# Attention and a mixture of experts on one core: when the last tokens' routing pieces are put between the expert matmuls

## The chip, the cores and the metric

The kernel runs on one core of a Trainium2 chip. A core has five engines with an instruction queue each: TensorE (matmuls; the profile writes PE, and PEld for its weight loads), VectorE (DVE), ScalarE (ACT), GpSimd (POOL) and SyncE (SP), which here issues transfers. An engine works through its queue in order; engines wait for each other by semaphores. The metric is the device time of one execution in microseconds, lower is better. Several executions are timed, and their median is compared; one further execution is recorded by the hardware profiler.

## The reference

Input is x of shape 8 x 1024 x 256, all in float32. There are two layers, each with a residual:

```python
x = x + layernorm(attention(layernorm(x)))      # 16 heads of 16, causal
x = x + layernorm(experts(layernorm(x)))

def experts(h):                                  # h: 8192 tokens x 256
    scores = softmax(h @ router_weight.T + router_bias)      # 8 experts
    topk_w, topk_idx = top_k(scores, 2)
    gu = einsum('th,ehn->ten', h, gate_up_proj) + gate_up_bias   # 2 x 512 columns
    gate, up = minimum(gu[..., :512], 7), clip(gu[..., 512:], -7, 7)
    act = (up + 1) * gate * sigmoid(1.702 * gate)
    down = einsum('tei,eih->teh', act, down_proj) + down_bias
    return weighted sum of the two chosen experts' rows of down
```

## The kernel before

**Two stages.** Attention goes through the 8 batches, 4 groups of heads each. Its output is projected, normalized and added per block of 512 tokens; there are 16 blocks (0 to 15), two for each batch. After it comes the expert stage. It computes only the chosen (token, expert) pairs: each token's normalized row is scattered to two rows of a table in DRAM (`xsd`), in which each expert has a region, and the expert stage reads this table in 71 tiles of 256 rows (`NTILES`), each belonging to one expert.

**The way of a block of tokens** (`finish`, L867, and `route`, L927 to L1052): output projection, normalization, residual; a second normalization to `xn`; transposes on TensorE (`x2ps`, L944), copied by ScalarE; the router's matmuls (`lpsT`, L951), a copy, a transpose (`lps`, L959); the softmax and the ranks of the experts on VectorE (L961 to L1001) ending in `is_r` and `chosen`; a matmul that counts the chosen ahead of each token (`cps`, L1005); ten small operations on VectorE that turn counts into rows (`counted`, `slot`, `counts`); then eight indirect scatters by GpSimd (L1046). For batch 7 (`last`), blocks 14 and 15, some pieces use other engines and other distances.

**The tables.** Which expert and which rows tile i takes is made on the chip (`table`, L279 to L366) from the counts: once from the first 12 blocks, for the first 12 tiles (`EARLY`), and once from all 16 for the rest. The second begins when block 15 is counted, after `fill_tails` (L252) has had the unused end of each expert's region filled with zeros: SyncE reads eight row numbers and issues eight transfers (L260). Then come the table's matmuls `segps` (L311), `firstps` (L319) and `tabps` (L343), each between small operations of VectorE. So the expert stage starts on rows of the first 12 blocks while batch 7's blocks are still on their way beside it.

**The order of work is written out.** TensorE, VectorE and ScalarE run in the order of the source, and GpSimd's instructions are held to it too. Side work is made of generators that yield pieces, each with its cost in us by engine and a distance:

```python
def piece(pe=0.0, dve=0.0, act=0.0, pool=0.0, after=0):
    return (pe, dve, act, pool), after
```

`pump(pe, dve, act, pool)` adds these amounts to a credit for each engine (capped at 0.9, GpSimd's at 1.3), then emits pieces whose engines are not in debt, and counts `now` up by one. A piece with `after=n` is not taken before n pumps have gone by since the piece ahead of it was emitted. The main loop of the expert stage calls `pump` three times in each quarter of a tile, as long as i + 2 < 12. At i = 10, `finish_all` emits what is left.

**An expert tile** (`quarter`, L1303; `lower_half`, L1335; loop L1453). A tile has four quarters (f = 0 to 3), of 128 gate and 128 up columns each: eight matmul records `gu` (L1308) into one of four PSUM buffers, with the first pump after half of them. VectorE makes `gate` (L1317) and `up` (L1321), ScalarE the sigmoid `sig` (L1319), GpSimd multiplies sig by gate (L1324); then the second pump. The product `act` (L1329) of the quarter before is issued on VectorE after that (`left()`), so that it is a quarter behind; after it stand the other work of the quarter and the third pump:

```python
                now_left = quarter(i, f, xT, wg, bs, act)
                if left:
                    left()
                left = now_left
```

After quarter 1 and after quarter 2 comes half of the previous tile's down product (`dn`, L1339), which needs its four `act`; after quarter 2 also the transposes of the next tile (`xtps`, L1288) and the operation `ys` (L1345) that empties `dn`. GpSimd scatters the result's rows (L1349).

**Loads.** SyncE loads tile i + 2 when tile i begins: its rows (`xs`, L1264), gate and up weights (`wg`, L1268; three buffers), biases (L1272) and down weights (L1276). The rows' load waits for the scatters into `xsd` that stand ahead of it in the source. The zeros stand in SyncE's queue between the loads of tile 9 and tile 10.

Side work and dn share three PSUM buffers (`ps_b`).

Of the kernel before, what the change touches and what calls it, by code (L numbers as in the profile page):

```python
# [24 lines left out]
def piece(pe=0.0, dve=0.0, act=0.0, pool=0.0, after=0):  # L25


    return (pe, dve, act, pool), after
# [30 lines left out]
def attn_moe_kernel(  # L59
# [179 lines left out]
    def ahead_of(load, group):  # L239

        tc.add_to_no_dep_group(group, load.ins)
# [37 lines left out]
    def table(nr):  # L279

        yield piece(dve=0.8)
        first_ones = nr < NT
# [22 lines left out]
        if first_ones:  # L305
            nc.vector.memset(new[:, nr:, :], 0.0)

        yield piece(pe=0.6, dve=0.2, after=3)
        ps = ps_b.tile([P, 2], F32, tag="b", name=f"segps_{nr}")
        for k, v in enumerate((new, nf[:, :NT, :])):  # L310
            nc.tensor.matmul(  # L311
# [26 lines left out]
        two = tp.tile([P, 2, NTILES], F32, tag="two", name=f"two_{nr}")  # L338
        nc.vector.tensor_scalar(two[:, 0, :], mine, seg_e, None, ALU.mult)
        nc.vector.scalar_tensor_tensor(two[:, 1, :], itile, at, mine, ALU.add, ALU.mult)  # L340
        yield piece(pe=0.5, dve=0.6, after=2)
        ps = ps_b.tile([P, 2, NTILES], F32, tag="b", name=f"tabps_{nr}")
        nc.tensor.matmul(  # L343
            ps.rearrange("o k i -> o (k i)"), lhsT=ones,
# [63 lines left out]
    with ExitStack() as attn:  # L408
# [123 lines left out]
        def others(wr):  # L532

            rwr, gubr = wr["r"], wr["gub"]

            nc.sync.dma_start(
                out=xs_dram[ds(E * R, TS), :].rearrange("(n p) d -> p n d", p=P), in_=zeros
            )
            for name in ("v", "o"):
                for kt in range(KT):  # L540
                    yield piece(pe=0.3, act=0.45)
                    weights(name, wr[name], kt)
            yield piece(pe=0.3, dve=0.2)
            ps = ps_b.tile([P, KT, E], F32, tag="b", name="rps")
            for kt in range(KT):
                nc.tensor.transpose(ps[:, kt, :], rwr[:, ts(kt, P)], ident[:E, :E])
            nc.vector.tensor_copy(rw32[:, :, :E], ps)
            yield piece(pe=0.2, dve=0.4)
            ps = ps_b.tile([P, E * 2 * FT], F32, tag="b", name="gubps")
            nc.tensor.transpose(ps, gubr, ident[: E * 2 * FT, : E * 2 * FT])  # L550
            bias = ap2.tile([P, E, 2 * FT], F32, tag="lgT", name="bias")
            nc.vector.tensor_copy(bias, ps.rearrange("p (e c) -> p e c", e=E))

            nc.vector.tensor_scalar(bias[:, :, FT:], bias[:, :, FT:], 1.0, None, ALU.add)
            nc.sync.dma_start(
                out=bias_dram[:, :, : 2 * FT].rearrange("e p c -> p e c"), in_=bias
            )
            for e in range(E):
                nc.sync.dma_start(
                    out=bias_dram[e, :, 2 * FT :], in_=down_b[e].partition_broadcast(P)  # L560
                )
# [365 lines left out]
        def route(t, x1, last):  # L927
# [10 lines left out]
            more = 1 if last else 0  # L938
# [5 lines left out]
                    nc.tensor.transpose(ps[:, n, :], xn[:, n, ts(kt, P)], ident)  # L944
                nc.scalar.copy(xT[:, kt, :], ps.rearrange("p n c -> p (n c)"))

            yield piece(pe=0.6, act=0.3, after=1 + more)
            ps = ps_b.tile([P, P], F32, tag="b", name=f"lpsT_{t}")
            for kt in range(KT):
                for n in range(NTB):  # L950
# [48 lines left out]
            for r in range(TOPK):  # L999
                nc.vector.tensor_scalar(is_r[:, r], rank, float(r), None, ALU.is_equal)  # L1000
            nc.vector.tensor_scalar(chosen, rank, float(TOPK), None, ALU.is_lt)  # L1001
            yield piece(pe=0.6, dve=0.2, after=1 + more)
            cps = ps_b.tile([P, 2, NTB, E], F32, tag="b", name=f"cps_{t}")
            for k, m in enumerate((before, ones)):
                nc.tensor.matmul(  # L1005
# [11 lines left out]
            for n in range(NTB):  # L1017
                nc.vector.tensor_tensor(slot[:, n, :], slot[:, n, :], so_far, ALU.add)
                after = counts[:, nth + 1, :]
                if n + 1 < NTB:  # L1020
                    after = small.tile([P, E], F32, tag="after", name="after")
# [43 lines left out]
        def start(kind, gen):  # L1065
            job = Job(gen, now)
            kind.append(job)
            return job
# [12 lines left out]
        def earn(*us):  # L1081
            for i, more in enumerate(us):
                credit[i] = min(credit[i] + more, 1.3 if i == 3 else 0.9)
# [9 lines left out]
        def spend(least=0.0, most=9.0):  # L1093


            found = affordable(least, most)
            if found:
                kind, job = found
                found = job.cost
                for i, cost in enumerate(job.cost):  # L1100
                    credit[i] -= cost
                emit(kind, job)
            return found

        def pump(*us, most=9.0):

            nonlocal now
            earn(*us)
            while True:
                got = spend(most=most)  # L1110
                if not got:
                    break

                if got[0] >= 0.3 and most <= 1.0:
                    most = min(most, 0.29)
            now += 1
# [22 lines left out]
        with tc.manual_schedule(  # L1139
# [5 lines left out]
            more = start(due, others(wr))  # L1145
# [157 lines left out]
    def quarter(i, f, xT, wg, bs, act):  # L1303

        ps = ps_gu.tile([P, 2, TS], F32, tag="gu", name=f"gu_{i}_{f}")
        for half in range(2):
            for kt in range(KT):
                nc.tensor.matmul(  # L1308
                    ps[:, half, :],
                    lhsT=wg[:, kt, ds(half * FF + f * P, P)],  # L1310
                    rhs=xT[:, kt, :],
                    start=(kt == 0), stop=(kt == KT - 1),
                )
            if half == 0 and i + AHEAD < EARLY:
                pump(0.6, 0.35, 0.6, 0.35)
        gt = m3.tile([P, TS], F32, tag="gate", name=f"gate_{i}_{f}")
        nc.vector.tensor_scalar(gt, ps[:, 0, :], bs[:, f : f + 1], LIMIT, ALU.add, ALU.min)  # L1317
        sg = m3.tile([P, TS], F32, tag="sig", name=f"sig_{i}_{f}")
        nc.scalar.activation(sg, gt, AF.Sigmoid, scale=ALPHA)  # L1319
        up = m3.tile([P, TS], F32, tag="up", name=f"up_{i}_{f}")  # L1320
        nc.vector.tensor_scalar(  # L1321
            up, ps[:, 1, :], bs[:, FT + f : FT + f + 1], LIMIT + 1.0, ALU.add, ALU.min
        )
        in_order(nc.gpsimd.tensor_tensor(sg, sg, gt, ALU.mult))  # L1324
        if i + AHEAD < EARLY:
            pump(0.6, 0.35, 0.6, 0.35)

        def product():
            nc.vector.scalar_tensor_tensor(  # L1329
                act[:, f, :], up, 1.0 - LIMIT, sg, ALU.max, ALU.mult  # L1330
            )

        return product
# [100 lines left out]
    with tc.manual_schedule(engines={engines.PE, engines.DVE, engines.Activation}):  # L1434
        free[0] = False
        loads = {0: load_tile(0)}
        for i in range(IN_X, 2 * IN_X):
            at = loaded(tables[NT - LATE][:, 1, i : i + 1], E * R)
            early[i] = m4.tile([P, TN, XD], F32, tag="xs", name=f"xs_{i}")
            ahead_of(nc.sync.dma_start(out=early[i], in_=slot_rows(at)), "xs")  # L1440
        for i in range(1, AHEAD):
            loads[i] = load_tile(i)
        xTs = {0: turned(0, loads[0][0])}
        behind, left = None, None
        waiting = deque()
        ready = 0
        ends = deque()

        def an_end(i):
            if ends and i >= ends[0][0] and next(ends[0][1], "end") == "end":  # L1450
                ends.popleft()

        for i in range(NTILES):  # L1453
            if i + AHEAD == EARLY:
                finish_all()
            if i + AHEAD < NTILES:
                loads[i + AHEAD] = load_tile(i + AHEAD)
            _, wg, bs, wd = loads.pop(i)
            xT = xTs.pop(i)
            act = m2.tile([P, FT, TS], F32, tag="act", name=f"act_{i}")  # L1460
            for f in range(FT):
# [4 lines that stand above are left out]
                for _ in range(2 if f == FT - 1 and i % 2 else 1):  # L1466
                    an_end(i)
                if f == 1 and behind:
                    next(behind)
                if f == 2:  # L1470
                    if i + 1 < NTILES:
                        xTs[i + 1] = turned(i + 1, loads[i + 1][0])
                    if behind:
                        next(behind)
                        next(behind)
                if i + AHEAD < EARLY:
                    pump(1.2, 0.7, 1.0, 0.7)
            while ready < NT and i >= tiles_for(ready):
                waiting.append(ready)
                ready += 1  # L1480
            if waiting and len(ends) < 2:
                work = both(routed[waiting.popleft()])
                next(work)
                ends.append((i + 2, work))
            behind = lower_half(i, act, wd, bs)
        left()
        for _ in behind:
            pass
        for r in [*waiting, *range(ready, NT)]:
            ends.append((0, both(routed[r], r == NT - 1)))  # L1490
        while ends:
            an_end(NTILES)
        free[0] = True
# [36 lines left out]
```

## Time and profile before

| what | value |
|---|---|
| median of 3 runs | 2231.09 us (2227.67 to 2233.11) |
| the profiled execution | 2227.21 us |
| its span, first to last instruction | 2225.5 us |
| TensorE busy | 2161.5 us, 97% of the span, 16801 matmul records |
| VectorE busy | 1647.3 us, 74% |
| ScalarE busy | 1090.8 us, 49% |
| GpSimd busy | 1067.0 us, 48% |
| expert stage's first `gu` | 1405.4 us from the span's start |
| `gu`, 2272 matmul records | 516.2 us, 379 ns each |
| `dn`, 1136 matmul records | 273.5 us, 381 ns each |
| scatters to `xsd`, 128 | 126.9 us, 992 ns each |

A busy time is the sum of the recorded durations on one engine, and matmul records overlap: one of 379 ns can be followed by the next after about 216 ns. Lines in order of time give start, duration, engine, line, operation, output and input, shape and count; what stands in brackets at the end is the engine's idle time ahead of it and what ended it. A wait's row names who waited for whom, the sum, how often, and the longest.

### The profile page before, as it was taken

The numbers are of one execution on the slowest core, as the hardware profiler recorded it, in microseconds if no ns is written. First come the engines' busy times: TensorE is split into PE (matmuls) and PEld (weight loads), VectorE is DVE, ScalarE is ACT, GpSimd is POOL, SyncE is SP. The second block draws the span as 40 slices with busy tenths as digits, with TensorE's granted clock in tenths as the row PEclk, the third lists the DMA queues.
The fourth block names the chain that finished last, engine by engine and source line by source line (L and its number), as shares of the span: only waits on it lengthen the run. The fifth ranks groups of instructions, "written<-read, shape, count | busy, mean of one in ns | idle before, by whom it ended". The sixth has DMA issues, their size and how long they took to land.

```text
span 2225.5 us, 45180 instructions
## 1 busy us (share of the span) xinstructions
PE 2161.5 (97%) x16801; PEld 1347.5 (61%) x16801; DVE 1647.3 (74%) x3770; ACT 1090.8 (49%) x2179; POOL 1067.0 (48%) x1229
## 2 busy tenths in 40 slices
PE   7999999999999999999999999999999999999995
PEld 3444544544544445445445444778888888888885
DVE  4776777867867777877776787676668888887775
ACT  3666665665666666666666666431122322322222
POOL 3421652662573573473472463464444444444543
PEclk9999999999999999999999999999999999999998
DMA  4001102102102111111111111657667778777773
GB/s 106 17 12 35 26 16 55 40 21 59 40 21 55 36 30 38 52 30 31 49 40 23 45 52 40 219 178 253 214 227 269 259 262 273 266 243 273 241 245 124
DMA packets 141363, 251.17 MB, mean 113 GB/s; under 512 B 17664, under 2 KB 103576, under 8 KB 139224
## 3 DMA queue, kind: packets, MB, share of 16 engines
q1 hardware_dynamic: 126968, 212.17, 30.5%
q0 software_dynamic: 12960, 35.54, 4.2%
q8 instruction: 133, 2.18, 0.4%
q14 instruction: 86, 0.70, 0.1%
q10 hardware_dynamic: 1216, 0.58, 0.1%
HBM read 175.74 MB, written 55.76 MB: 104 GB/s over the span
## 4 chain that ended last, share of the span: by engine, by line
PE 81%; DVE 10%; POOL 4%; issue 3%; ACT 1%; DMA 1%; SPq 0%; ACTq 0%; DVEq 0%; POOLq 0%
PE sa L693 20%; PE gu L1308 17%; PE av L825 12%; PE dn L1339 9%; PE sb L788 7%; PE yps L886 3%; PE pjq L600 3%; PE pjk L600 3%; PE vps L586 2%; PE avt L856 1%; DVE acc L1391 1%; PE xtps L1288 1%; DVE gate L1317 1%; DVE act L1329 1%; DVE up L1321 1%
## 5 line engine op out<-in xcount | busy, mean ns | idle before, releaser
L796 ACT ACTIVATE pT<-sb 128x512 f32<-128x512 f32 x1152 | 625.2, 595 | 404.5 <-PE sb L788 375.7
L788 PE MATMUL sb<-qP,kP 32*128 32x512 f32 (+3 forms) x3072 | 710.7, 523 | 2.1 <-DMA qP<-nmT 1.0
L693 PE MATMUL sa<-kP,qP 32*128 32x512 f32 (+3 forms) x3072 | 653.8, 524 | 3.4 <-DVE mx L703 1.4
L1308 PE MATMUL gu<-xsT,wg 128*128 128x256 f32 x2272 | 516.2, 379 | 0.8 <-ACT xsT L1290 0.7
L1308 PEld LDWEIGHTS gu<-xsT,wg 128*128 128x128 f32 x2272 | 430.6, 190 | 59.9 <-ACT xsT L1290 1.4
L805 POOL TENSOR_SCALAR_AFFINE_SELECT pT<-pT 128x512 f32<-128x512 f32 x256 | 160.0, 641 | 592.3 <-ACT pT L796 586.9
L709 DVE TENSOR_REDUCE mx<-sa 128x2 f32<-128x1024 f32 x256 | 311.5, 1219 | 112.2 <-PE sb L788 108.6
L1319 ACT ACTIVATE sig<-gate 128x256 f32<-128x256 f32 x284 | 118.3, 417 | 562.7 <-DVE gate L1317 560.7
L825 PE MATMUL av<-pT,vpad 128*32 128x256 f32 (+1 forms) x5120 | 345.0, 366 | 1.1 <-DVE avs L836 0.9
L1324 POOL TENSOR_TENSOR sig<-sig,gate 128x256 f32<-128x256 f32 x284 | 210.6, 743 | 274.9 <-ACT sig L1319 273.0
L693 PEld LDWEIGHTS sa<-kP,qP 32*128 32x128 f32 x3072 | 227.8, 184 | 188.4 <-issue 97.3
L788 PEld LDWEIGHTS sb<-qP,kP 32*128 32x128 f32 x3072 | 297.6, 184 | 40.9 <-ACT pT L796 7.2
L825 PEld LDWEIGHTS av<-pT,vpad 128*32 128x32 f32 x5120 | 116.4, 108 | 287.2 <-issue 208.0
L1339 PE MATMUL dn<-wd,act 128*128 128x256 f32 x1136 | 273.5, 381 | 8.0 <-DVE act L1329 7.5
L1317 DVE TENSOR_SCALAR gate<-gu,bs 128x256 f32<-128x256 f32 x284 | 135.7, 478 | 154.2 <-PE gu L1308 138.1
L1339 PEld LDWEIGHTS dn<-wd,act 128*128 128x128 f32 x1136 | 208.6, 190 | 40.7 <-DVE act L1329 16.0
L703 DVE CUSTOM_DVE_ANT_0 sa<-sa,cmask 128x512 f32<-128x512 f32 x256 | 178.1, 697 | 51.2 <-PE sb L788 27.0
L1349 POOL DMA_INDIRECT ytd<-ys,places x142 | 142.9, 1006 | 136.5 <-DVE ys L1345 112.3
L1046 POOL DMA_INDIRECT xsd<-xn,slots x128 | 126.9, 992 | 47.0 <-issue 29.4
L718 DVE TENSOR_REDUCE mx<-sa 128x2 f32<-128x512 f32 x128 | 88.1, 689 | 75.5 <-PE sb L788 49.7
L1329 DVE SCALAR_TENSOR_TENSOR act<-up,sig 128x256 f32<-128x256 f32 x284 | 131.7, 464 | 14.5 <-POOL sig L1324 14.5
L1321 DVE TENSOR_SCALAR up<-gu,bs 128x256 f32<-128x256 f32 x284 | 134.5, 474 | 0.0
(204 smaller groups left out, 2399.9 us busy)
## 6 DMA issues: line engine op xcount, KB each, us to landing
wg<-_L_ffn_gate_up_proj_dram SPq DMA_DIRECT2D x71, 1024.0 KB
wd<-in_L_ffn_down_proj_dram SPq DMA_DIRECT2D x71, 512.0 KB
xs<-xsd SPq DMA_DIRECT2D x67, 258.0 KB
yy<-ytd SPq DMA_DIRECT2D x15, 1024.0 KB
bs<-biasd SPq DMA_DIRECT2D x71, 132.0 KB
x<-in_L_attn_x_dram SPq DMA_DIRECT2D x16, 512.0 KB
x1d<-y SPq DMA_DIRECT2D x16, 512.0 KB
x<-x1d SPq DMA_DIRECT2D x16, 512.0 KB
```

Source lines behind the costliest of these rows:

```text
L693: nc.tensor.matmul(ps[:, hh, ds(at, w)], lhsT=qP[r, ts(i, P)], rhs=kP[r, ds(c * QC, w)], start=True, stop=True,)
L703: nc.vector.tensor_tensor_reduce(out=ps[:, hh, :], in0=ps[:, hh, :], in1=cmask, scale=1.0, scalar=NEG, op0=ALU.add, op1=ALU.max, accum_out ...
L709: nc.vector.tensor_reduce(mx[:, heads, i, 2:3], ps, AX.X, ALU.max)
L788: nc.tensor.matmul(banks[hh][:, ds(at, QC - off)], lhsT=kP[r, ts(j, P)], rhs=qP[r, ds(c * QC + off, QC - off)], start=True, stop=True,)
L796: nc.scalar.activation(pT[:, 2 * pair + hh, :], banks[hh], AF.Exp)
L805: in_order(nc.gpsimd.affine_select(out=d, in_=d, compare_op=ALU.is_ge, fill=0.0, base=0, pattern=[[0, HG], [1, P]], channel_multiplier=-1,))
L825: nc.tensor.matmul(av[ds(hh * HS, HS), ds(off + a - at, z - a)], lhsT=vp[:, j, ds((g * HG + hh) * VS, HS)], rhs=pT[:, hh, a:z],  start=c n ...
L1308: nc.tensor.matmul(ps[:, half, :], lhsT=wg[:, kt, ds(half * FF + f * P, P)], rhs=xT[:, kt, :], start=(kt == 0), stop=(kt == KT - 1),)
L1317: nc.vector.tensor_scalar(gt, ps[:, 0, :], bs[:, f : f + 1], LIMIT, ALU.add, ALU.min)
L1321: nc.vector.tensor_scalar(up, ps[:, 1, :], bs[:, FT + f : FT + f + 1], LIMIT + 1.0, ALU.add, ALU.min)
L1324: in_order(nc.gpsimd.tensor_tensor(sg, sg, gt, ALU.mult))
L1339: nc.tensor.matmul(ps[:, n, :], lhsT=act[:, f, ts(n, P)], rhs=wd[:, f, :], start=(f == 0), stop=(f == FT - 1),)
```

## The change

Six numbers change, and with them the order in which the pieces of blocks 14 and 15 and of the second table are emitted. For `last` blocks the router's matmul `lpsT` gets a distance of 3 pumps instead of 2, and `cps` 5 instead of 2; for the second table `segps` gets 5 instead of 3 and `tabps` 5 instead of 2. Other blocks and the first table keep theirs. Of the three pumps of a quarter, the two inside `quarter` add nothing to VectorE's credit (0.35 each before), and the third, after the product, adds 1.4 instead of 0.7. No instruction is added or removed.

```diff
 def table(nr):
-        yield piece(pe=0.6, dve=0.2, after=3)
+        yield piece(pe=0.6, dve=0.2, after=3 if first_ones else 5)
         ps = ps_b.tile([P, 2], F32, tag="b", name=f"segps_{nr}")
...
-        yield piece(pe=0.5, dve=0.6, after=2)
+        yield piece(pe=0.5, dve=0.6, after=2 if first_ones else 5)
         ps = ps_b.tile([P, 2, NTILES], F32, tag="b", name=f"tabps_{nr}")
...
 def route(t, x1, last):
-            yield piece(pe=0.6, act=0.3, after=1 + more)
+            yield piece(pe=0.6, act=0.3, after=1 + 2 * more)
             ps = ps_b.tile([P, P], F32, tag="b", name=f"lpsT_{t}")
...
-            yield piece(pe=0.6, dve=0.2, after=1 + more)
+            yield piece(pe=0.6, dve=0.2, after=1 + 4 * more)
             cps = ps_b.tile([P, 2, NTB, E], F32, tag="b", name=f"cps_{t}")
...
 def quarter(i, f, xT, wg, bs, act):
             if half == 0 and i + AHEAD < EARLY:
-                pump(0.6, 0.35, 0.6, 0.35)
+                pump(0.6, 0.0, 0.6, 0.35)
...
         if i + AHEAD < EARLY:
-            pump(0.6, 0.35, 0.6, 0.35)
+            pump(0.6, 0.0, 0.6, 0.35)
...
                 if i + AHEAD < EARLY:
-                    pump(1.2, 0.7, 1.0, 0.7)
+
+                    pump(1.2, 1.4, 1.0, 0.7)
```

## The prediction

> **What bounds the kernel now.** I read the page's slices first, then the waits of TensorE in the stretch that the change reaches, then the rows in order of time of TensorE, VectorE and GpSimd there. The page, TensorE's share of the 40 slices and the chain that ended last:
>
> ```profile
> PE   7999999999999999999999999999999999999995
> ...
> PE 81%; DVE 10%; POOL 4%; issue 3%; ACT 1%; DMA 1%; SPq 0%; ACTq 0%; DVEq 0%; POOLq 0%
> ```
>
> TensorE is the bound throughout, so the change is worth what TensorE waits less. The instructions differ only between the expert stage's start (1405 us) and tile 10 (about 1534 us); before and after it, every engine has the old order. TensorE's waits from 1395 to 1545 us (line, who ended it, sum, times, longest):
>
> ```profile
> PE cps L1005 <- DVE chosen L1001: 3.1, 2, 2.1
> PE dn L1339 <- DVE act L1329: 2.9, 3, 1.4
> PE tabps L343 <- DVE two L340: 2.1, 1, 2.1
> PE segps L311 <- DVE new L304: 1.2, 1, 1.2
> PE lpsT L951 <- ACT xT L945: 1.0, 1, 1.0
> ```
>
> All five belong to the last tokens' way (blocks 14 and 15, then the table) or to the products of an expert tile. Sum 10.3 us. How much is it with the cost of stopping and starting? Busy time by stage, from the first quarter of tile 2 to that of tile 9, beside an undisturbed stretch (TensorE, weight loads, VectorE, ScalarE, GpSimd, clock, DMA):
>
> ```profile
> 1428.70:1523.00 94.30, 83.66 (x432) 70.22 (x432) 74.39 (x227) 28.43 (x58) 55.48 (x62) 1.00 0.62 202
> 1523.00:1599.00 76.00, 76.00 (x368) 66.93 (x367) 45.40 (x113) 14.99 (x35) 34.63 (x43) 1.00 0.68 236
> ```
>
> **What can be had at most.** An undisturbed tile takes 10.80 us (tile 8's last quarter starts at 1521.24, tile 9's at 1532.04): 1.73 for each of four quarters and two halves of the down product, 0.43 for the transposes. Seven tiles are 75.6. The other pieces in between, start to start: four transposes x2ps 1.74, two lpsT 1.16, two lps 0.24, two cps 0.88, segps, firstps and tabps 0.91, in all 4.9. The floor is 80.5 against 94.3: **13.7 us lost**. Idle by the row is 94.30 - 83.66 = 10.6. Here the Trainium skill (Perfetto Trace Analysis, Identifying the Most-Contended Engine) says that matmul busy time is no measure of headroom, and to take the weight loads' share: 70.22/94.30 = 0.745 against 66.93/76 = 0.881 gives 94.3 x (1 - 0.745/0.881) = 14.6 us. Idle alone would miss 3 us. I take my count from starts, 13.7: about 0.25 us more than its idle time for each stop, and some 0.1 for each small product between large ones, which stays (0.7). So 13 us is the ceiling.
>
> **The change, part by part** (times on the old clock; tile i, quarter f).
>
> *VectorE's pieces behind the product.* The two pumps inside a quarter no longer earn VectorE credit; its 1.4 us all come after the product (L1329). Same pieces, later by up to a third of a quarter.
> - Tile 1's down product waits 1.15 us for act of f=3. In the new order one sum (L900, 0.37) is gone from before gate of f=2, and a pair of statistics (0.53) from between up and act. act ends at about 1433.9 instead of 1435.1; TensorE wants it at 1432.56 + 6 x 0.216 = 1433.86. Left: 0.1.
> - Transposes x2ps of block 14 now get their shift (L915) behind ys, about 1.2 us later; ScalarE's last normalization ends at about 1442.1, TensorE wants it at 1442.1. I take 0.1 (0 to 0.6).
>
> *Longer distances.* lpsT leaves the middle of tile 3's quarter 1 for behind half of tile 2's down product: 2 x 1.73 us after x2ps, while ScalarE's two copies take 1.05. Its 1.0 goes. cps of block 14 goes from behind quarter 0 of tile 4 to behind quarter 2, three groups (5.2 us) later; chosen is done long before. Its 0.92 goes. cps of block 15 (2.13) moves from tile 5, quarter 2, to tile 6, quarter 0. Between rank and chosen stand a product, far, ys and the two comparisons; chosen ends about 1478.5, TensorE arrives at 1478.05. Left: 0.5 (0 to 1.2). segps and tabps move two, and four and a half, such groups back; new and two, which they wait for, move one back: 1.2 and 2.1 go. The table is then known about when tile 9 begins; it is read by SyncE for tile 12, whose load in the old run issues behind tile 9.
>
> ```profile
> 1472.53 0.19 DVE L975 TENSOR_REDUCE lsm<-sc 128x4 f32<-128x32 f32 x1 [1.36 <-ACT sc L970]
> ...
> 1476.25 0.97 DVE L991 TENSOR_TENSOR ge<-ge,lower 128x256 f32<-128x256 f32 x1
> 1477.26 0.83 DVE L993 TENSOR_TENSOR ge<-ge,gt 128x256 f32<-128x256 f32 x1
> ...
> 1500.75 0.43 DVE L1329 SCALAR_TENSOR_TENSOR act<-up,sig 128x256 f32<-128x256 f32 x1 [1.51 <-POOL sig L1324]
> ```
>
> *Tile 4's down product* (1.45) was late because VectorE stood 1.36 us for the exponential and ScalarE reloaded its table behind it. In the new order a product, far, ys (1.7 us) or more lie between the subtraction and the sum; both loads (1.28 each way, as many as before) fall elsewhere. act of f=3 comes at 1469.6, wanted at 1470.2. Left: 0.
>
> *Tile 5's* gets worse: the ten small counting operations behind cps (1.74 us, 1461.08 to 1462.82 for block 14) now stand before act of f=3. 0.34 becomes 0.8 (0.3 to 1.8).
>
> *GpSimd, tiles 5 to 7.* Behind these products stands GpSimd: each sig (0.74) queues behind the token scatters. From the first scatter of block 14 to sig of tile 7, f=3, it has 16 scatters x 1.22, six result scatters x 1.3 and twelve sig x 0.74 = 36.2 us; the old run took 39.1:
>
> ```profile
> 1472.31 0.96 POOL L1046 DMA_INDIRECT xsd<-xn,slots  x1 [0.30 <-issue]
> ...
> 1510.69 0.73 POOL L1324 TENSOR_TENSOR sig<-sig,gate 128x256 f32<-128x256 f32 x1
> ```
>
> It is nearly full, so here TensorE cannot gain freely. The first scatter starts 3.2 us earlier (1469.1: two waits and their restarts are gone by then, block 14's columns are ready at 1468.4). With 37.5 us for the chain, sig of tile 7 ends at 1506.6. Tile 6's down product then waits 0.75 (0 to 1.8; 0.2 before), tile 7's 1.0 (0 to 2; none before).
>
> A rule speaks against the change here: the Trainium skill (SBUF - State Buffer, Who interferes with whom) has a VectorE instruction with two SBUF inputs and a GpSimd one that reads SBUF shut each other out for a whole instruction. Pieces behind the product fall beside scatters. The row: the four comparisons of block 15 took 2.63 us beside scatters, 1.45 at their undisturbed pace, 0.3 more each. If each were shut out for a scatter (1.0) it would be 4.0, tile 5's act 2.8 later still, and the gain below 5.7 instead of 8.5. I take the row, which is this same overlap.
>
> *SyncE.* Tails (L255, L257) come a quarter later, behind ys of tile 7, quarter 2: at about 1500.0. Their eight fills with zeros (SyncE, 1.29 us apart) stand behind the loads of tile 9, which wait for a scatter of block 15 (the fourth, it was the fifth) and end about 1499.4 (1506.0 before). Behind the fills stand tile 10's rows, which wait for the last fill:
>
> ```profile
> 1506.56 9.45 SPq L260 DMA_DIRECT2D xsd<-zeros  x8
> 1522.31 0.40 SPq L1264 DMA_DIRECT2D xs<-xsd  x1
> ```
>
> From tile 9's rows (1503.57) to tile 10's (1522.31) are 18.7 us, nearly all with the DMA engines full. From 1496.9 this gives about 1516.2; with some 3 us to land (packets of it flow until about 1525 in the old run), 1519.2. TensorE wants them at about 1520. Left: 0 (0 to 2); the old run had some 4 us to spare. Tile 8's rows and tile 10's weights keep several us.
>
> **Sum.** Remaining waits 0.1 + 0.1 + 0.5 + 0.8 + 0.75 + 1.0 = 3.25, six stops at 0.2 more: 4.5. Gain 13 - 4.5 = **8.5 us**. The profiled execution took 2227.21 with a span of 2225.5: 2217.0 + 1.7 = 2218.7. The median of the runs, 2231.09, lies 3.9 higher: **2222.6 us**, 0.38% faster. About 0.3% (6.7 us) is what a measurement of this kernel tells from no change.
>
> **Rivals.**
> 1. *GpSimd keeps its pace* and the waits only change their names: the chain still takes 39.1 us and starts 1.5 us earlier. Tile 7's product then ends about 4 us earlier, and segps and tabps, already freed, add nothing. Gain 4: 2227. For it: GpSimd's idle gaps were under 1 us each. Against: they sum to 2, and TensorE's saving before the first scatter is plain. 0.22.
> 2. *Tile 10's rows late behind the zeros*: fills held up by later tails, landing at 1522.5 against 1520. Gain 5 to 6: 2226. 0.07.
> 3. *Slower*: act waits for sig in VectorE's order, and behind it now stand all the pieces that make GpSimd's next scatters; gate and up of the next quarter queue there too. If each of the twelve products of tiles 5 to 7 waits for a pair of scatters (2 us), that is 24 - 13 = 11 us more: 2242. It decides from (13 + 6.7)/12 = 1.6 us each on. The old run has 1.5 and 0.9 as its worst waits of this kind. 0.08.
> 4. *Nothing*: the planner's banked credit puts pieces inside quarters all the same (the counting group of tile 6 shows it). But the built order did move the five waits. Gain 0 to 2: 2230. 0.03.
>
> **How the numbers follow.** Likeliest case 0.60, its own range 2219 to 2226. Range 2218.5 to 2230: rivals 1, 2 and 4 are in, rival 3 and a little at each end are out. Faster: 0.53 from the likeliest case and 0.03 from rivals 1 and 2. Slower: rival 3, 0.08. Within: 0.36.
>
> **What would show it.** After: no wait at lpsT, segps, tabps; cps at most once and under 1.2; the down product's waits for act about as large as before (2 to 4 us), now in tiles 5 to 7; tile 9's first quarter starts near 1514.5; first scatter of block 14 near 1469; no wait at xtps. Wrong: waits at act over 1.6 us each, or a wait at xtps or gu for a load in tiles 9 and 10.

## The result and the profile after

The changed kernel takes **2221.46 us** (median of 7 runs, 2219.76 to 2226.29) against 2231.09 (7 runs, 2226.53 to 2235.58): the ratio recorded for the two sets of runs is **0.9965, 95% interval 0.9954 to 0.9976**, so 7.8 us (5.3 to 10.3) or 0.35% faster. It is not quite the ratio of the two medians, which differ by 9.6 us. The profiled execution took 2221.46 with a span of 2219.7, 5.8 less than before's 2225.5, both at a mean granted clock of 0.994.

The page of the changed kernel, TensorE's share of the slices and the chain that ended last:

```profile
PE   7999999999999999999999999999999999999995
...
PE 80%; DVE 10%; POOL 5%; issue 3%; ACT 1%; DMA 1%; SPq 0%; ACTq 0%; DVEq 0%; POOLq 0%
```

A change of this size does not show on the page. It shows in the waits of TensorE from 1395 to 1545 us (line, who ended it, sum, times, longest):

```profile
PE dn L1339 <- DVE act L1329: 3.9, 5, 1.3
PE gu L1308 <- ACT xsT L1290: 1.3, 2, 0.7
PE xtps L1288 <- DVE avs L836: 0.8, 1, 0.8
PE lps L959 <- ACT lgT L956: 0.3, 1, 0.3
PE x2ps L944 <- ACT xn L921: 0.2, 1, 0.2
```

cps, tabps, segps and lpsT, 7.4 us before, are gone from the list. The down product's waits rose from 2.9 to 3.9, and one wait at gu (0.59; the other, 0.67, is tile 0's in both kernels) is new. The windows of the two stretches, from the first quarter of tile 2 to that of tile 9, and the undisturbed one after it (columns as in the prediction):

```profile
1429.15:1517.63 88.48, 83.49 (x431) 70.21 (x431) 73.42 (x223) 28.18 (x58) 54.76 (x61) 1.00 0.66 213
1517.63:1593.60 75.97, 75.97 (x368) 66.92 (x367) 46.31 (x116) 14.98 (x35) 35.01 (x43) 1.00 0.69 239
```

94.3 us became 88.5: all 5.8 us of the span's difference were saved here. Busy time is the same (83.66 and 83.49); idle time fell from 10.6 to 5.0. Where the rest of it stands, TensorE in order of time:

```profile
1435.14 0.70 PE L1339 MATMUL dn<-wd,act 128*128 128x256 f32 x2 [0.69 <-DVE act L1329]
...
1479.99 1.99 PE L1308 MATMUL gu<-xsT,wg 128*128 128x256 f32 x8 [0.59 <-ACT xsT L1290]
1486.11 0.70 PE L1339 MATMUL dn<-wd,act 128*128 128x256 f32 x2 [0.66 <-DVE act L1329]
1498.23 0.70 PE L1339 MATMUL dn<-wd,act 128*128 128x256 f32 x2 [1.05 <-DVE act L1329]
...
1511.01 0.70 PE L1339 MATMUL dn<-wd,act 128*128 128x256 f32 x2 [1.27 <-DVE act L1329]
```

These are the down product of tile 1, the first quarter of tile 6, and the down products of tiles 5, 6 and 7. GpSimd's first token scatter of block 14 and its last sig of tile 7:

```profile
1472.17 1.01 POOL L1046 DMA_INDIRECT xsd<-xn,slots  x1 [0.56 <-DVE xn L1042]
...
1509.26 1.41 POOL L1324 TENSOR_TENSOR sig<-sig,gate 128x256 f32<-128x256 f32 x2
```

The last row holds two multiplies; the first of them, which ends at 1509.99, is tile 7's. The scatters begin when they did before (1472.31); the chain to that sig takes 37.8 us instead of 39.1. And SyncE, the fills with zeros and tile 10's rows:

```profile
1504.79 9.19 SPq L260 DMA_DIRECT2D xsd<-zeros  x8
1520.89 0.40 SPq L1264 DMA_DIRECT2D xs<-xsd  x1
```

Tile 10's transposes start at 1524.5 without a wait, 3.65 us after the issue of their rows (7.6 before).

### The profile page after: what moved, and what is told of

Same layout as the page of the kernel before. It is cut to its first block, busy times and chain, and to the rows that moved or that the text cites. A ratio compares the mean times of both kernels' runs of the same rounds, so it can differ in the third digit from the quotient of the medians.

```text
span 2219.7 us, 45179 instructions
## 1 busy us (share of the span) xinstructions
PE 2161.7 (97%) x16801; PEld 1348.1 (61%) x16801; DVE 1647.0 (74%) x3770; ACT 1090.6 (49%) x2179; POOL 1067.7 (48%) x1229
## 4 chain that ended last, share of the span: by engine, by line
PE 80%; DVE 10%; POOL 5%; issue 3%; ACT 1%; DMA 1%; SPq 0%; ACTq 0%; DVEq 0%; POOLq 0%
PE sa L693 20%; PE gu L1308 17%; PE av L825 12%; PE dn L1339 8%; PE sb L788 7%; PE yps L886 3%; PE pjq L600 3%; PE pjk L600 3%; PE vps L586 2%; PE avt L856 1%; DVE acc L1391 1%; DVE gate L1317 1%; PE xtps L1288 1%; DVE act L1329 1%; POOL pT L805 1%
```

## The experiments

The expected effects are 1 to 5 us. The start of the expert stage alone moves by more than that from execution to execution: tile 1's transposes began between 1413.8 and 1420.4 us in eleven executions on chips of like speed, with the same instructions before them. So the yardstick below is a stretch of one execution: **from the start of tile 1's transposes to that of tile 13's** (rows of xtps, TensorE in order of time). What the change moves ahead of it costs nothing: from the first `gu` to tile 1's transposes are 10.12 or 10.13 us in every trace. Where nothing is in the way, a tile takes 10.80 in every one of them. There is one trace of each kernel, so no stretch was measured twice; what can be said is that waits which should be alike are (tile 1's product with the old pumps: 1.15, 1.15, 1.15 and 1.16 in four kernels). "Waits" adds up TensorE's waits of 0.15 us or more within it. Each experiment's ratio is to runs of the kernel before on the same chip. The diffs of 1 to 4 and of 11 are against the changed kernel, the others against the run that the text names.

| kernel | stretch, us | waits, us | ratio to before (95%) |
|---|---|---|---|
| before | 146.77 | 10.4 | 1 |
| changed | 140.96 | 4.9 | 0.9965 (0.9954 to 0.9976) |
| 1 distances alone | 141.46 | 4.9 | 0.9972 (0.9962 to 0.9982) |
| 2 pieces behind the product alone | 142.37 | 4.7 | 0.9969 (0.9958 to 0.9980) |
| 3 no multiply in tiles 5 to 7 | 136.13 | 1.0 | 0.9939 (0.9926 to 0.9951) |
| 4 scatters apart and spread | 138.82 | 2.9 | 0.9959 (0.9946 to 0.9972) |
| 5 as 1, tails and table apart | 141.13 | 4.5 | 0.9975 (0.9967 to 0.9984) |
| 6 as 5, behind in tiles 0 to 3 | 142.10 | 5.8 | 0.9975 (0.9963 to 0.9987) |
| 7 as 6, scatters spread | 143.40 | 5.6 | 0.9983 (0.9975 to 0.9991) |
| 8 as 7, fills split | 138.25 | 3.0 | 0.9961 (0.9948 to 0.9973) |
| 9 as 8, loads without the wait | 136.52 | 1.4 | 0.9951 (0.9937 to 0.9964) |
| 10 as 9, old pumps | 139.70 | 3.3 | 0.9970 (0.9960 to 0.9981) |
| 11 multiply kept, not read | 139.38 | 3.1 | 0.9956 (0.9938 to 0.9973) |
| 12 as 9, behind everywhere | 138.66 | 2.9 | 0.9939 (0.9924 to 0.9955) |

Two rows hold a loss that is no wait: in 2 and in 7 the granted clock of TensorE fell to 0.50 within the stretch, for 3.4 and 6.8 us. In the other twelve traces it is 1.00 throughout. By the matmuls that ran slower this cost about 1.7 and 2.1 us (an estimate, worked out below).

**1. The distances alone.**

```diff
-pump(0.6, 0.0, 0.6, 0.35)      # both pumps inside a quarter
+pump(0.6, 0.35, 0.6, 0.35)
-pump(1.2, 1.4, 1.0, 0.7)
+pump(1.2, 0.7, 1.0, 0.7)
```

> The four longer distances alone (lpsT, cps, segps, tabps), the pumps of the kernel before. My theory, that the distances make the gain: they take away 1.0 + 3.1 + 1.2 + 2.1 of the waits, tile 1's down product keeps its 1.1 for act, tile 5 to 7 keep 2 to 3 behind GpSimd; stretch from tile 2's first quarter to tile 9's 89 to 90 us (94.3 before, 88.5 in the changed kernel), time 4 to 5 us below before. Rival, that VectorE's pieces behind the product make it: the waits at cps and tabps only shrink to half, stretch 92 to 93, time 1 to 2 us below before.

**2. VectorE's pieces behind the product alone.**

```diff
-yield piece(pe=0.6, dve=0.2, after=3 if first_ones else 5)   # segps
+yield piece(pe=0.6, dve=0.2, after=3)
-yield piece(pe=0.5, dve=0.6, after=2 if first_ones else 5)   # tabps
+yield piece(pe=0.5, dve=0.6, after=2)
-yield piece(pe=0.6, act=0.3, after=1 + 2 * more)             # lpsT
+yield piece(pe=0.6, act=0.3, after=1 + more)
-yield piece(pe=0.6, dve=0.2, after=1 + 4 * more)             # cps
+yield piece(pe=0.6, dve=0.2, after=1 + more)
```

> VectorE's pieces behind a product alone, the four distances of the kernel before. My theory: the waits at cps, segps and tabps stay (6 us) and grow a little, because what they wait for now comes later; only the products of tile 1 and 4 gain, stretch 93 to 95 us, time within 2 us of before. Rival: stretch 90 to 91, time 3 to 4 us below before.

The first saved 5.3 us, the second 4.4, which my theory didn't allow. (In the window that the expectations name, tile 2's to tile 9's first quarter, they took about 87 and 90 us; the first is below its 89 to 90 because the table's last matmul and the two late loads below fall behind that window.) **The theory that the distances alone make the gain fell**: either half takes most of it, and together they give 5.8, not 9.7. The waits of TensorE in the second experiment, from 1395 to 1545 us, show how:

```profile
PE cps L1005 <- DVE chosen L1001: 1.7, 1, 1.7
PE firstps L319 <- DVE seg L316: 1.5, 1, 1.5
...
PE dn L1339 <- DVE act L1329: 0.7, 1, 0.7
...
PE segps L311 <- DVE new L304: 0.4, 1, 0.4
```

With the old distances, the later VectorE pieces by themselves put cps of block 14 and tabps in places where nothing is waited for, and tiles 4 to 7 have no wait at the down product at all. The two halves remove the same waits, and a wait goes only once. The second would have saved more at a steady clock, as TensorE's rows show:

```profile
1482.62 0.41 PE L1005 MATMUL cps<-chosen,before 128*128 128x32 f32 x2 [1.69 <-DVE chosen L1001]
...
1483.09 3.58 PE L1308 MATMUL gu<-xsT,wg 128*128 128x256 f32 x8
```

Eight `gu` take 1.89 us elsewhere. From 1483.09 to 1486.47 the granted clock is 0.53; the 1.7 us that this costs would bring the second to about 6.1 us saved, as much as both halves together. That the stop of 1.69 us brought the slow clock about is not shown: the kernel before has two stops of 2.1 us with a clock of 1.00.

In the first experiment cps, segps, tabps and lpsT show no wait, tile 1 keeps its 1.15 and tiles 5 to 7 have 2.05. But it has two waits more, at tile 11's rows and weights, which neither theory named: they stand behind six of the eight fills on SyncE.

```profile
1537.87 0.63 PE L1288 MATMUL xtps<-ident,xs 128*128 128x128 f32 x4 [0.95 <-DMA xs<-xsd]
1542.42 2.83 PE L1308 MATMUL gu<-xsT,wg 128*128 128x256 f32 x12 [0.46 <-DMA wg<-_L_ffn_gate_up_proj_dram]
```

**3. Without GpSimd's multiply.** In tiles 5 to 7 the product takes ScalarE's sig without the factor gate.

```diff
-in_order(nc.gpsimd.tensor_tensor(sg, sg, gt, ALU.mult))
+if not 5 <= i <= 7:
+    in_order(nc.gpsimd.tensor_tensor(sg, sg, gt, ALU.mult))
```

> The changed kernel, but in tiles 5, 6 and 7 GpSimd doesn't multiply sig by gate (the product takes sig as ScalarE leaves it, so these tiles' activations are another function). My theory, that GpSimd behind the scatters makes act late in tiles 6 and 7: their waits of 1.05 and 1.27 go, tile 5's (0.66, the counting group ahead of act) stays at 0.4 or more, stretch 85.5 to 86.5 against 88.5, time 2 to 3 us below the changed kernel. Rival, that VectorE's own pieces make act late: both waits stay over 0.5, stretch above 87.5, time within 1 us of the changed kernel.

The waits of tiles 6 and 7 went, but so did tile 5's 0.66 and gu's 0.59, and the stretch fell by 4.8 us, twice what I expected, with no more than 1.0 us of waits left. So all four hang on GpSimd, tile 5's too. VectorE in order of time, the comparisons of block 15, in the changed kernel

```profile
1473.93 0.95 DVE L988 TENSOR_TENSOR ge<-sc 128x256 f32<-128x256 f32 x1
...
1476.26 0.97 DVE L991 TENSOR_TENSOR ge<-ge,lower 128x256 f32<-128x256 f32 x1
1477.27 0.84 DVE L993 TENSOR_TENSOR ge<-ge,gt 128x256 f32<-128x256 f32 x1
...
1479.59 0.70 DVE L1293 TENSOR_SCALAR far<-xs 128x2 f32<-128x2 f32 x1
```

and in the third experiment

```profile
1473.72 0.42 DVE L988 TENSOR_TENSOR ge<-sc 128x256 f32<-128x256 f32 x1
...
1475.52 0.42 DVE L991 TENSOR_TENSOR ge<-ge,lower 128x256 f32<-128x256 f32 x1
1475.97 0.42 DVE L993 TENSOR_TENSOR ge<-ge,gt 128x256 f32<-128x256 f32 x1
...
1477.88 0.16 DVE L1293 TENSOR_SCALAR far<-xs 128x2 f32<-128x2 f32 x1
```

while GpSimd scatters beside them without a pause (the same experiment):

```profile
1473.27 0.96 POOL L1046 DMA_INDIRECT xsd<-xn,slots  x1 [0.30 <-issue]
1474.54 0.96 POOL L1046 DMA_INDIRECT xsd<-xn,slots  x1 [0.30 <-issue]
1475.80 0.96 POOL L1046 DMA_INDIRECT xsd<-xn,slots  x1 [0.30 <-issue]
```

**It is the multiply, not the scatter, that holds VectorE up.** The first comparison took 0.42 in both. The small operations that count block 15 are held up too: from the copy of cps to act of quarter 3 VectorE takes 2.19 us in the changed kernel and 1.48 in the third experiment. The experiment removes two things at once, the wait of act for sig and this hold-up; experiment 11 parts them.

**4. The scatters apart and spread.**

```diff
+def to_slots():                     # the scatters of blocks' tokens, as they were
...
+if last:
+    start(back, to_slots())
+else:
+    yield from to_slots()
...
-pump(0.6, 0.0, 0.6, 0.35)
+pump(0.6, 0.0, 0.6, 0.35 if i < 4 else 0.0)
-pump(1.2, 1.4, 1.0, 0.7)
+pump(1.2, 1.4, 1.0, 0.7 if i < 4 else 1.05)
```

> The changed kernel with the scatters of blocks 14 and 15 as a job of their own, so that tails and table don't stand behind them, and from tile 4 on GpSimd's pieces only behind a product, one a quarter, spread to tile 8 or 9. My theory: a sig stands behind one scatter at most; waits of tile 6 and 7 fall from 2.3 to under 0.8, stretch 86.5 to 87.5, time 1 to 2 us below the changed kernel. Rival, that the same scatters cost the same wherever they stand: the waits only move to tiles 8 and 9, stretch to tile 10 unchanged, time within 0.7 us of the changed kernel.

Tiles 6 and 7 lost their waits (2.3 us to none), as my theory says. Tile 5's rose from 0.66 to 1.26 and gu's stayed at 0.59. The stretch is 2.1 us shorter, just above what I expected. The ratios' intervals overlap, so by the whole time alone it isn't shown to be faster than the changed kernel.

**5 to 7. Where the pieces behind the product help.** The fifth is the first with the scatters as a job of their own (`to_slots` above). The sixth adds VectorE's pieces behind the product in tiles 0 to 3. The seventh spreads the scatters as in 4.

```diff
-pump(0.6, 0.35, 0.6, 0.35)                      # 5
+pump(0.6, 0.0 if i < 4 else 0.35, 0.6, 0.35)    # 6; in 7 the last is 0.35 if i < 4 else 0.0
-pump(1.2, 0.7, 1.0, 0.7)
+pump(1.2, 1.4 if i < 4 else 0.7, 1.0, 0.7)      # in 7 the last is 0.7 if i < 4 else 1.05
```

> The first experiment (four distances, old pumps) with the scatters of blocks 14 and 15 as a job of their own with the same GpSimd credit, so that tails and table no longer stand behind them: the eight fills then come before the loads of tile 9. Theory A, that the first experiment lost 1.4 us of waits and 2 us of stretch in tile 11 to rows and weights behind the fills: both waits on DMA go, tile 1's to tile 13's transposes take 139 to 140 us (141.5 in the first experiment, 141.0 in the changed kernel), so that the distances without the moved pieces are better than with them. Theory B, that the loads are late for another reason: the wait at tile 9, 10 or 11 comes back, 141 to 142 us.

> As the one before, and VectorE's pieces behind the product in tiles 0 to 3 alone (there nothing scatters tokens). Theory A, that pieces behind the product help where GpSimd is free and harm where act waits for it: tile 1's down product gains 0.46, tiles 5 to 7 stay as in the run before (waits for act 2.0 to 2.6 in all), tile 1's to tile 13's transposes 138.3 to 139.5 us. Theory B, that the late pieces harm through the order they give blocks 14 and 15, not through GpSimd: tiles 5 to 7 are as bad as in the changed kernel (3 us of waits at the down product and 0.6 at gu), 140.5 us or more.

> As the one before, and from tile 4 on GpSimd's pieces only behind a product, about one scatter a quarter (they then reach to tile 7's end). If the scatters ahead of each sig are what is left, the waits of tiles 5 to 7 fall from 2.3 to about 1, tile 1's to tile 13's transposes take 137 to 138 us, time 3 us below the changed kernel (ratio to before 0.994 to 0.996). If the scatters cost as much one by one, the stretch stays at 138.5 or more.

All three missed their stretches, mainly for one reason. The waits at the down product and at gu for act and xsT did fall from step to step: in tiles 5 to 8 to 1.7 in the fifth, 1.2 in the sixth, none in the seventh. But with tails and table no longer behind the scatters, the eight fills now stand ahead of tile 9's rows, and the earlier TensorE gets there, the longer it waits: 0.31 and 0.88 at rows and weights in the fifth, 1.32 and 1.59 in the sixth, 4.15 in the seventh. SyncE in order of time, and the wait on TensorE, in the seventh:

```profile
1491.06 10.36 SPq L260 DMA_DIRECT2D xsd<-zeros  x8
1511.41 0.40 SPq L1271 DMA_DIRECT2D xs<-xsd  x1
```

```profile
1514.63 1.08 PE L1295 MATMUL xtps<-ident,xs 128*128 128x128 f32 x4 [4.15 <-DMA xs<-xsd]
1515.51 3.62 PE L1346 MATMUL dn<-wd,act 128*128 128x256 f32 x8
```

The rows are issued 10 us after the last fill, of which 9.2 are a wait for the fills, and land 3 us later. In the seventh this stop came with a slow clock: from 1514.6 to 1519.0 us it was 0.50, the four transposes took 1.08 us (0.60 elsewhere) and the eight `dn` 3.62 (1.89), 2.1 us more from start to start. That is the "some 2" that the next expectation puts down to late rows. The theory that the fills delay the rows holds; that moving them forward by a tile would end it was wrong. Theory B of the sixth fell: tiles 5 to 7 were better, not as bad as in the changed kernel.

**8. The fills split.** The code asks for up to three fills behind each tile's loads; on SyncE they stand as four behind the loads of tile 8 and four behind those of tile 9, two tiles earlier than the expectation says.

```diff
-for e in range(E):                   # in fill_tails
-    at = loaded(itail[0:1, e : e + 1], E * R)
-    apart(nc.sync.dma_start(out=slot_rows(at), in_=zeros), "xs")
+fills.extend((itail, e) for e in range(E))
...
     loads[i + AHEAD] = load_tile(i + AHEAD)
+    some_fills(3)                    # up to three of them, the same two lines each
```

> As the run before (pieces behind the product in tiles 0 to 3 alone, one scatter a quarter from tile 4), but the eight fills with zeros are no longer issued where the counts are known: four stand behind the loads of tile 10 and four behind those of tile 11. Theory A, that what tiles 8 to 10 lost there (4.15 us at tile 9's rows and some 2 after them) is rows that wait for the last fill: no wait on DMA at tiles 9 to 12, tile 1's to tile 13's transposes take 136.5 to 137.5 us (143.4 before, 141.0 in the changed kernel), time 4 us below the changed kernel, ratio to before 0.9945 to 0.9965. Theory B, that the DMA engines themselves are full then, whatever the order: 1 us or more of waits comes at the rows or weights of tiles 10 to 12, stretch 138.5 to 141.

5.1 us better than the seventh, of which 2.1 are the clock. What stays is 1.31 at tile 10's rows, as theory B has it, but SyncE's waits name a cause ahead of the DMA engines (line, what it waited for, sum, times, longest, from 1500 to 1575 us):

```profile
SPq L1277 <- DMA xsd<-xn,slots: 30.8, 4, 16.7
...
SPq L1277 <- DMA xsd<-zeros: 2.2, 1, 2.2
```

The loads of the tiles' rows wait for token scatters that were issued before them, though these tiles' rows come from other blocks.

**9. Loads without that wait.** The rows of tiles 8 to 11 were written by the first twelve blocks, before tile 0's load; the wait on later scatters protects nothing there.

```diff
-if i < EARLY:
+if 4 <= i < EARLY:
+    apart(load, "xs")
+elif i < EARLY:
     ahead_of(load, "xs")
```

> As the eighth experiment, and the rows of tiles 8 to 11, which come from the first twelve blocks, no longer wait on SyncE for the token scatters of blocks 14 and 15 or for the fills. There these waits (16.7 us the longest, 33 in all) pushed the loads of tiles 9 and 10 and the fills into one stretch. Theory A: with the loads at their own time no transposes wait for rows; tile 1's to tile 13's transposes take 136.3 to 137.0 us (138.3 there, 141.0 in the changed kernel), ratio to before 0.994 to 0.996. Theory B, that the DMA engines are full whatever SyncE waits for: 1 us or more of waits on rows or weights stays in tiles 9 to 12, 138 or more.

Theory A: no wait on DMA, 136.52 us. All waits of TensorE from 1395 to 1560 us (the one at avs and 0.68 of xsT are tile 0's, as in every run):

```profile
PE dn L1354 <- DVE act L1344: 1.3, 2, 0.7
PE xtps L1303 <- DVE avs L842: 0.8, 1, 0.8
PE gu L1323 <- ACT xsT L1305: 0.7, 1, 0.7
PE x2ps L950 <- ACT xn L927: 0.2, 1, 0.2
```

This is the best that came of it by the stretch: 10.25 us less than before, 4.4 less than the changed kernel; the medians on the same chip are 2218.86 us against 2230.52, the recorded ratio of the runs is 0.9951.

**10. The same with the old pumps**, both VectorE's and GpSimd's credit as before.

```diff
-pump(0.6, 0.0 if i < 4 else 0.35, 0.6, 0.35 if i < 4 else 0.0)
+pump(0.6, 0.35, 0.6, 0.35)
-pump(1.2, 1.4 if i < 4 else 0.7, 1.0, 0.7 if i < 4 else 1.05)
+pump(1.2, 0.7, 1.0, 0.7)
```

> As the ninth, but with the old pumps throughout (VectorE and GpSimd credit inside the quarters and behind): the four distances without the pieces behind the product, and no row late. Theory A, that the moved pieces cost more in tiles 5 to 7 than they gain in tile 1: 138.5 to 139.5 us (waits for act about 2.5, gu 0.6), 1.5 to 2.5 less than the changed kernel's 141.0, and 2 more than the ninth. Theory B, that they are worth something once rows are in time: 141.0 or more.

139.70: 1.3 less than the changed kernel and 3.2 more than the ninth. Theory B fell, and theory A's range was missed by 0.2. With the rows in time, the distances without the moved pieces are no worse than the changed kernel. But this kernel also has tails and table apart, so the 1.3 isn't the pumps' alone; and it differs from the ninth in GpSimd's credit too, so neither are the 3.2.

**11. The multiply kept, but not read.** The product takes sig as ScalarE leaves it, as in 3.

```diff
+if 5 <= i <= 7:
+    spare = m1.tile([P, TS], F32, tag="spare", name=f"spare_{i}_{f}")
+    in_order(nc.gpsimd.tensor_tensor(spare, sg, gt, ALU.mult))
+else:
     in_order(nc.gpsimd.tensor_tensor(sg, sg, gt, ALU.mult))
```

> The changed kernel, but in tiles 5, 6 and 7 GpSimd writes sig times gate to a spare tile that nothing reads, and the product takes sig as ScalarE leaves it (these tiles' activations are another function, as in the third experiment). GpSimd's work and its order are those of the changed kernel; only VectorE no longer waits for it. Theory A, that act waiting in VectorE's order for a sig behind scatters makes the waits of tiles 5 to 7: they go as in the third experiment, tile 1's to tile 13's transposes take 136 to 137 us (141.0 in the changed kernel, 136.1 there). Theory B, that it is VectorE's instructions held up while GpSimd multiplies (0.3 to 0.6 us each in the rows, 15 times in tiles 5 to 7): these stay and with them tile 5's 0.66 and gu's 0.59, 139 to 140 us; tile 6 and 7 alone get better.

Theory B. Tiles 6 and 7 have no wait left; tile 5's and gu's are there (TensorE in order of time; on this chip the expert stage begins some 34 us later):

```profile
1513.91 1.99 PE L1308 MATMUL gu<-xsT,wg 128*128 128x256 f32 x8 [0.59 <-ACT xsT L1290]
1520.11 0.70 PE L1343 MATMUL dn<-wd,act 128*128 128x256 f32 x2 [0.74 <-DVE act L1333]
```

The comparisons took 0.96, 0.97 and 0.83 again. So **two mechanisms**: in tiles 6 and 7 act waits in VectorE's order for a sig that stands behind scatters (gone in 3, 4 and 11); in tile 5 VectorE itself is late, because its pieces in a row are held up by multiplies (gone in 3, there in 4 and 11). Of the 3.25 us that 139.38 still holds over the third's 136.13, 1.3 are these two waits, 0.46 a wait at tile 8's down product, where act reads the multiply's result again and the scatters aren't over, and 0.23 one for tile 10's weights. At 0.2 for each of the four stops, some 0.4 stay without a name.

**12. The ninth with the pieces behind the product everywhere.**

```diff
-pump(0.6, 0.0 if i < 4 else 0.35, 0.6, 0.35 if i < 4 else 0.0)
+pump(0.6, 0.0, 0.6, 0.35 if i < 4 else 0.0)
-pump(1.2, 1.4 if i < 4 else 0.7, 1.0, 0.7 if i < 4 else 1.05)
+pump(1.2, 1.4, 1.0, 0.7 if i < 4 else 1.05)
```

> The ninth experiment with VectorE's pieces behind the product in all of tiles 0 to 9, as in the changed kernel, and not in tiles 0 to 3 alone. Theory A, that these late pieces are what costs in tile 5 (the comparisons of block 15 and the counting group in a row ahead of gate and act): 138.3 to 139.3 us from tile 1's to tile 13's transposes against 136.5, waits at tile 5's down product about 1.2 and at the first quarter of tile 6 about 0.6, as in the fourth experiment. Theory B, that once scatters are spread the place of VectorE's pieces doesn't matter: under 137.2.

```profile
1509.92 1.99 PE L1323 MATMUL gu<-xsT,wg 128*128 128x256 f32 x8 [0.57 <-ACT xsT L1305]
1516.66 0.70 PE L1354 MATMUL dn<-wd,act 128*128 128x256 f32 x2 [1.28 <-DVE act L1344]
```

Theory A: 138.66, 2.1 us more than the ninth, at the two places named (TensorE in order of time, above). The whole time doesn't show this: the ratio, 0.9939, is even below the ninth's, with intervals that overlap. The runs made together on this chip had a mean granted clock of 0.9905 for this kernel and 0.9879 for the one before; among the latter the time falls by 17.7 us for each 0.01 of clock, so by this estimate 4.6 of the 13.8 us go with the clock, and 9.2 stay against 8.1 by the stretch.

## Why the prediction was right, and where it wasn't

**The time was right (2222.6 forecast, 2221.46 measured), the sum behind it 2.7 us too good.** The stretch gained 5.8 us, not 8.5. That the median of the runs came within 1.2 us of the forecast is partly luck: it moved by 9.6 us, and the ratio of the runs, 7.8 us (5.3 to 10.3), holds both 5.8 and 8.5. The mechanism was right in its first half: the five waits on the last tokens' way went, and what remained stood in tiles 5 to 7 behind GpSimd. Its size was not, and it is to be judged by the stretch. Tile 9's first quarter came at 1517.63, 1514.5 was forecast.

- *The ceiling was nearly right.* I counted 80.5 us for seven tiles with all pieces. From tile 3's transposes to tile 10's, seven tiles with the same pieces, the ninth experiment took 82.69 (before 92.45, changed 87.14) with 0.74 of waits in two stops left. Less these and 0.2 for each stop it is 81.55; I had 80.5 and 0.7 unavoidable, 81.2.
- *What a stop costs besides its wait, 0.2 us, holds.* Between the changed kernel and the third experiment five waits went, 3.82 us in all (0.25 at lps, 0.59, 0.66, 1.05, 1.27), and 4.83 us were gained: 0.2 for each. I counted six remaining stops; there were eight, as many as before. So none of that cost went with the change.
- *The distances:* no wait at lpsT, segps, tabps and block 14's cps, as predicted; block 15's cps had none either (0.5 said). Right, but experiment 2 shows that I gave them sole credit for what the later pieces also do.
- *Tile 1's product:* 0.1 predicted, 0.69 measured: the mis-sized term of this part. The sum and the statistics did leave its way; act of quarter 3 then waited 0.22 for sig and took 0.98 instead of 0.42, beside the next multiply.
- *Tile 4's product:* 0 predicted, 0.19 measured. *x2ps:* 0.1 and 0.17.
- *Tile 5's product:* 0.8 predicted, 0.66 measured, near by luck: **the step left out half of the cause**. I put it down to the counting group ahead of act. That group stands there in the third experiment too, and there is no wait. In the changed kernel the group itself is held up by a multiply, 0.71 us from the copy of cps to act, and VectorE comes to it late from the stretched comparisons; by the rows either of the two is about the whole wait. The comparisons also delayed gate of quarter 2, by it the sig and behind that ScalarE's copy xsT, and so gu of tile 6: 0.59 that I hadn't listed.
- *Tiles 6 and 7:* 0.75 and 1.0 predicted, 1.05 and 1.27 measured. The mechanism, sig behind scatters on a nearly full GpSimd, is what 3, 4 and 11 show.
- *GpSimd's chain:* 37.5 us predicted, 37.8 measured. (The 36.2 counted twelve sig; thirteen stand in the chain in both kernels, which makes 36.9.) Its start was wrong: 1469.1 predicted, 1472.17 measured, no earlier than before (1472.31). I took the time that TensorE saves as time that the scatters come earlier; but the columns that they wait for (L1042) are VectorE pieces, which the other half of the change moves later. Rival 1 (the chain keeps its 39.1 us) was wrong in its premise and nearer in its gain, 4 us against the 5.8 measured.
- *SyncE:* tails predicted at 1500.0, measured at 1504.28, since ys of tile 7, behind which they stand, came only at 1503.28; tile 10's rows at 1516.2, measured at 1520.89. (1516.2 counts from the fills; from tile 9's rows at 1496.9 the sum is 1515.6.) No wait, as predicted, but because TensorE was late by as much: luck. Rival 2, tile 10's rows late behind the fills, had 0.07; late loads on SyncE beside the fills are what met five of the experiments (1 and 5 to 8), up to 4.15 us in the seventh.
- *The rule weighed:* I took the row, 0.3 us more for each comparison, "beside scatters". The size held for the four instructions that I counted (L990 to L994: 2.64 us, as before), not the 4.0 of a shut-out for each. But two of them were stretched, by 0.56 and 0.43, and two not at all; without the multiply the four take 1.68, not 1.45; and the partner was wrong: it is the multiply. That 5.8 came out near the 5.7 which I gave for the full shut-out is chance.
- *Rival 3 (slower):* its threshold was 1.6 us for each of twelve products. The two longest waits of act for sig were 2.62 and 2.57, over the 1.6 that I had named as a sign of being wrong; but there were seven in all, 7.4 us, of which 2.3 reached TensorE in tiles 6 and 7.

In the sum, remaining waits 3.25 became 4.87 (tile 1 +0.6, gu +0.6, tiles 6 and 7 +0.6, lps and tile 4 +0.4, cps -0.5, the others -0.1) and two stops more +0.4: 2.0 of the 2.7. The remaining 0.7 is the ceiling's, by estimate: 88.48 less the 4.87 of waits and 0.2 for each of eight stops leaves 82.0, and 94.3 less 82.0 is 12.3 us to be had, not 13.

## What to carry to other kernels

Give a piece a longer distance only as far as its wait asks for, and look at what its producer's engine does next: two edits that free the same wait don't add up, and what they move can bunch on another engine. Before packing vector work behind one instruction, count the GpSimd instructions that will run beside it. When a stage gets faster, the transfers with the least slack are next; list their slack before, and keep bulk fills away from the loads of the next tiles. Where a stretch is longer than its waits explain, read the granted clock within it.

## What the runs showed of the hardware that I had not expected

**VectorE is held up by GpSimd's multiply and not by its scatters.** From 1440 to 1560 us of the changed kernel 25 VectorE instructions took over 0.2 us more than the shortest of the same line in the trace, 12.3 us in all, and all 25 overlap a sig multiply (before: 20 of 20). A comparison of 128x2 elements (L1293), 0.16 us by itself, took 0.70, as long as the multiply (0.73) beside it. The scatters alone held up next to nothing (two instructions in the third experiment, by 0.2 each). The Trainium skill (SBUF - State Buffer, Who interferes with whom) has an exclusive lock between a VectorE instruction with two SBUF inputs and a GpSimd instruction that reads SBUF: 14 of the 25 are of this kind and behave so. The other eleven, L1293 among them, read one tile of SBUF and are held up as well. I had let the scatters count as such GpSimd instructions; the runs don't show it of them.

**Run-to-run scatter on one chip goes with the granted clock.** Over 49 runs of the kernel before on one chip the mean granted clock lay between 0.989 and 0.996, and the time falls by 17 us for each 0.01 of it. Chips differ by more: on two with a mean of 0.988 the kernel before took 2265 and 2268 us, on three with 0.992 to 0.993 about 2230, of which that slope explains 9 us at most. In the traces from the two slower chips the stage before the experts ends some 34 us later; why is open. A gain of a few us is better read in a stretch of the trace than in whole times.
